# Edge counts in four quarters of a block, source one-hots in unwritten penalty slices, and attention columns formed after block 5

## The chip, the cores and the metric

The kernel runs on one core of one Trainium2 chip. The metric is the device time of one execution in microseconds (us). TensorE multiplies matrices, VectorE, ScalarE and GpSimd work on elements, and SyncE (SP) issues DMA transfers. Each engine takes its instructions in a fixed order of its own; semaphores tie the engines together.

## The reference

Two graph attention layers and a feed-forward part with residuals, over 1250 nodes of 768 features and 21250 edges sorted by target node:

```python
def gat_layer(x, W, att_src, att_dst, bias, src, dst, heads, out_ch, concat):
    h = (x @ W.T).reshape(n, heads, out_ch)
    a_src = jnp.einsum('nhc,hc->nh', h, att_src)
    a_dst = jnp.einsum('nhc,hc->nh', h, att_dst)
    e = jax.nn.leaky_relu(a_src[src] + a_dst[dst], 0.2)
    m = jax.ops.segment_max(e, dst, num_segments=n)
    ex = jnp.exp(e - m[dst])
    denom = jax.ops.segment_sum(ex, dst, num_segments=n)
    alpha = ex / (denom[dst] + 1e-16)
    out = jax.ops.segment_sum(alpha[:, :, None] * h[src], dst, num_segments=n)
...
x = x + gnn(layernorm(x), ...)    # gat 8 heads x 128, relu, gat 1 head x 768
x = x + ffn(layernorm(x)[None], ...)[0]
```

## The kernel before

The edge lists are turned into a dense matrix of counts: entry (target, source) says how many edges join the two. The 1250 nodes are ten blocks of 125 and the edges 170 chunks of 125, so that a block has 17 chunks (`CPB`) on average. For every chunk the kernel makes two one-hot matrices with one edge per partition: a source one-hot `of` over all 1250 nodes (VectorE, line 233) and a target one-hot `to` over the few nodes the chunk can reach (VectorE for the first 36 chunks; after that every third on GpSimd, line 249, the rest on ScalarE in two steps, lines 254 and 257). A matmul of `to` against `of` adds the chunk's edges to the counts of a block in PSUM (line 275).

Because the edges are sorted, a chunk touches only a few target nodes. `WINDOWS` (line 57) says which chunks are multiplied into which half of a block: two halves of 64 columns, 13 chunks each, laid over one another by a margin. One round of `count_block` (line 260) takes one chunk for each half, in three slices of the sources (512, 512 and 226); the two halves are two column tiles of TensorE's array. Edges outside their windows are counted (`n_out`, line 218), and if there is one, `count_all` (line 302) does all counts again without windows; with these inputs that branch is not taken, but all engines meet at it (line 558).

When a block's counts are complete, `use_count` (line 281) has ScalarE copy them to `full`, write the penalties `absent[:, b]` (zero where there is an edge, a huge number where there is none, line 286) and, after TensorE's transposes (line 297), the transposed counts `ct`. `absent` is one tile of ten slices of 1250 bf16 values, a slice for each block.

The softmax's maximum is found from the largest source term of each target: `top_of_block` (line 501) subtracts the penalties from a row of source terms and takes the maximum, one VectorE instruction for each head and block (line 503, which the profile lists as `unused<-rows,absent`). The rows of source terms come by way of memory: `a1p` (line 437) gives them for all heads, ScalarE copies them to `a1_row`, SP stores them to `as1_d` (line 446) and reads each head's row back, broadcast over partitions (line 492). The same `a1_row` is transposed into columns `a1` (lines 449 to 460: three transposes, five copies), from which `low_high` makes two scaled sets (line 480). The columns are first read by `load_destination_rows` and by the weights of the heads, all behind the branch.

The first stage runs: count block 0, layer norm and transposes of the ten blocks of `x`, `a1p`, the columns, and then for blocks 1 to 9 `count_block`, `h1_block(0, b)` (the features of heads 0 to 3, line 387) and the maxes named in `behind`. The `of` tiles rotate through 11 buffers, the `to` tiles through 13. The framework fixes the order on each engine when the kernel is built: it is not the program's order throughout, and maxes and one-hots are mixed on VectorE. Behind the branch come `load_destination_rows` for head 0 (its transpose `r_h_p`, line 465, and the copy `r_h_s`, line 467), four blocks of `h1` for heads 4 to 7, and the heads' loop, in which VectorE makes the weights (lines 527 and 531) and TensorE sums over sources (line 685).

Of the kernel before, what the change touches and what calls it, by code (L numbers as in the profile page):

```python
# [26 lines left out]
BF16 = mybir.dt.bfloat16  # L27
F16 = mybir.dt.float16
# [6 lines left out]
N = 1250  # L35
D = 768
E = 21250
H1, C1 = 8, 128
# [4 lines left out]
B = 125  # L43
NB = N // B
EC = E // B
# [7 lines left out]

CPB = EC // NB
MARGIN = 2
HALF = 64
WINDOWS = (
    (-MARGIN, -(-CPB * HALF // B) + MARGIN), (CPB * HALF // B - MARGIN, CPB + MARGIN)
)

NW = N + 128 - B + 1
# [4 lines left out]
def gnn_ffn(  # L66
# [25 lines left out]
    nc = tc.nc  # L92
# [15 lines left out]
    def ps_tr(name):  # L108
        return psum.tile([128, 512], F32, tag="tr", bufs=2, name=name)
# [16 lines left out]
    ep = pool("early", stack=early)  # L126
# [38 lines left out]
    first_i = ep.tile([B, NB, CPB], I32, name="first_i")  # L165
    last_i = ep.tile([B, NB, CPB], I32, name="last_i")

    def halves_of(r):

        return [  # L170
            2 * o + j for o in (-1, 0, 1) for j in range(2)
            if WINDOWS[j][0] <= r - CPB * o < WINDOWS[j][1]
        ]

    def start_of(half):
        return half // 2 * B + half % 2 * HALF

    for t, bounds in (
        (first_i, [start_of(halves_of(r)[0]) for r in range(CPB)]),
        (last_i, [start_of(halves_of(r)[-1] + 1) for r in range(CPB)]),  # L180
    ):
        c0 = 0
        for c1 in range(1, CPB + 1):
            if c1 == CPB or bounds[c1] != bounds[c0]:
                nc.gpsimd.iota(
                    t[:, :, c0:c1], pattern=[[B, NB], [0, c1 - c0]], base=bounds[c0],
                    channel_multiplier=0,
                )
                c0 = c1
# [3 lines left out]
    absent = marks.tile([B, NB, N], BF16, tag="marks", name="absent")  # L193
# [5 lines left out]
    ident = const.tile([128, 128], F32, name="ident")  # L199
# [8 lines left out]
    src_f = ep.tile([B, EC], F32, name="src_f")  # L208
# [17 lines left out]
    node = ep.tile([B, NW], F16, name="node")  # L226
# [1 line left out]
    minus_dst = ep.tile([B, EC], F32, tag="edge", name="minus_dst")  # L228
    nc.vector.tensor_scalar(minus_dst, dst_f, -1.0, None, op0=OP.mult)  # L229

    def one_hot(name, col, nodes, tag, bufs):
        t = ep.tile([B, nodes.shape[-1]], BF16, tag=tag, bufs=bufs, name=name)
        nc.vector.tensor_scalar(t, nodes, col, None, op0=OP.is_equal)  # L233
        return t


    hot = {}

    def hot_chunk(c):

        halves = [h + c // CPB * 2 for h in halves_of(c % CPB)]
        halves = [h for h in halves if 0 <= h < 2 * NB]
        of = one_hot(f"of{c}", src_f[:, c : c + 1], node[:, :N], "of", 11)
        n0 = start_of(halves[0])
        w = start_of(halves[-1]) + HALF - n0
        to = ep.tile([B, 3 * HALF], BF16, tag="to", bufs=13, name=f"to{c}")
        if c < 2 * CPB + MARGIN or c % 3 == 0:
            eng = nc.vector if c < 2 * CPB + MARGIN else nc.gpsimd
            eng.tensor_scalar(  # L249
                to[:, :w], node[:, n0 : n0 + w], dst_f[:, c : c + 1], None, op0=OP.is_equal  # L250
            )
            return of, to, n0
        away = ep.tile([B, 3 * HALF], F16, tag="away", bufs=1, name=f"away{c}")
        nc.scalar.activation(  # L254
            away[:, :w], node[:, n0 : n0 + w], AF.Abs, bias=minus_dst[:, c : c + 1], scale=1.0
        )
        nc.scalar.activation(to[:, :w], away[:, :w], AF.Relu, bias=ones, scale=-1.0)  # L257
        return of, to, n0

    def count_block(b):  # L260

        p = ps_count(f"count{b}")
        spans = [(max(0, CPB * b + lo), min(EC, CPB * b + hi)) for lo, hi in WINDOWS]
        for i in range(max(hi - lo for lo, hi in WINDOWS)):
            now = [(j, CPB * b + WINDOWS[j][0] + i) for j in range(2)]
            now = [(j, c) for j, c in now if spans[j][0] <= c < spans[j][1]]
            for _, c in now:
                if c not in hot:
                    hot[c] = hot_chunk(c)
            for c0 in range(0, N, 512):  # L270
                c1 = min(N, c0 + 512)
                for j, c in now:
                    of, to, n0 = hot[c]
                    o = start_of(2 * b + j) - n0
                    nc.tensor.matmul(  # L275
                        p[HALF * j : HALF * (j + 1), c0:c1], to[:, o : o + HALF], of[:, c0:c1],
                        start=(c == spans[j][0]), stop=(c == spans[j][1] - 1),
                    )
        use_count(p[:B, :N], b, f"w{b}", F16)

# [21 lines left out]
    def count_all():  # L302

        count = absent.bitcast(U16)
        nc.vector.memset(count, 0)
        with tc.For_i(0, EC, 1) as c:
            cols = ep.tile([B, 2], F32, name="cols")
            for i, t in enumerate((src_f, dst_f)):
                nc.vector.tensor_copy(cols[:, i : i + 1], t[:, bass.ds(c, 1)])
            of = one_hot("g_src", cols[:, 0:1], node[:, :N], "of", 11)  # L310
            to = one_hot("g_dst", cols[:, 1:2], node[:, :N], "of", 11)
            for b in range(NB):
                p = ps_count(f"g_count{b}")
                for c0 in range(0, N, 512):
                    c1 = min(N, c0 + 512)
                    nc.tensor.matmul(
                        p[:B, c0:c1], to[:, b * B : (b + 1) * B], of[:, c0:c1], start=True, stop=True
                    )
                nc.vector.tensor_tensor(count[:, b], p[:B, :N], count[:, b], OP.add)
        for b in range(NB):  # L320
            use_count(count[:, b], b, f"g{b}")
# [74 lines left out]
    for g in range(2):  # L396
        for h in range(H1):
            j = h % 4
            nc.tensor.matmul(
                vt[g][32 * j : 32 * j + 32, :384], att[:, h], w1n[h // 4][:, h % 4, g * 384 : (g + 1) * 384],  # L400
                start=(h < 4), stop=(h >= 4),
# [9 lines left out]
    p = ps_tr("vp")  # L411
    for k in range(KD):
        nc.tensor.matmul(
            p[:, 32 * k : 32 * k + 32], vt_s[:, k * 128 : (k + 1) * 128], pick_head,
            start=True, stop=True,
# [17 lines left out]
    spans = [(0, 3), (3, 6), (6, 8), (8, 10)]  # L433
    p = ps_mm("a1p")
    for k in range(KD):
        for j, (b0, b1) in enumerate(spans):
            nc.tensor.matmul(
                p[32 * j : 32 * j + 32, : (b1 - b0) * B], v[:, k], xt[:, k, b0 * B : b1 * B],
                start=(k == 0), stop=(k == KD - 1),
            )  # L440
    a1_row = ep.tile([128, 3 * B], F32, name="a1_row")
# [3 lines left out]
    for j, (b0, b1) in enumerate(spans):  # L445
        nc.sync.dma_start(
            as1_d[:, b0 * B : b1 * B], a1_row[32 * j : 32 * j + H1, : (b1 - b0) * B]
        )
    p = ps_tr("a1tp")
    a1 = const.tile([B, 2, H1, NB], F32, name="a1")  # L450
    for i in range(3):
        n = 128 if i < 2 else 64
        nc.tensor.transpose(
            p[:B, 128 * i : 128 * i + n], a1_row[:n, i * B : (i + 1) * B], ident[:n, :n]
        )
        pv = p[:B, 128 * i : 128 * i + n].rearrange("p (j c) -> p j c", c=32)[:, :, : 2 * H1]
        pv = pv.rearrange("p j (t h) -> p t h j", t=2)
        nc.vector.tensor_copy(a1[:, :, :, i : i + 4 : 3], pv[:, :, :, :2])
        if i < 2:
            nc.vector.tensor_copy(a1[:, :, :, 6 + i : 9 + i : 2], pv[:, :, :, 2:])  # L460

    def rows_to_dram(cols, n, name, sp):

# [8 lines left out]
    def low_high(a_s, shape, name):  # L472

        lo = const.tile(shape, F32, name=f"{name}_lo")
        nc.vector.tensor_scalar(lo, a_s, SLOPE, None, op0=OP.mult)
        hi = const.tile(shape, F32, name=f"{name}_hi")
        nc.vector.tensor_scalar(hi, a_s, 1.0 - SLOPE, None, op0=OP.mult)
        return lo, hi

    as1_lo, as1_hi = low_high(a1[:, 0], [B, H1, NB], "as1")  # L480


    class Head:
# [61 lines left out]
    def first_tops(blocks, hs=range(EARLY)):  # L545
        for b in blocks:
            for h in hs:
                top_of_block(heads[h], b)

    behind = {3: (0, 1), 4: (2,), 5: (3,), 6: (4,), 7: (5, 6), 8: (7,), 9: (8,)}  # L550
    for b in range(1, NB):
        count_block(b)
        if b == 1:
            h1_block(0, 0)
        h1_block(0, b)
        first_tops(behind.get(b, ()), range(4))
    first_tops(range(4), [4])
    with tc.If(n_val > 0):  # L558
        count_all()
# [115 lines left out]
    for h in range(H1):  # L675
        hd = heads[h]
        acc = [ps_mm(f"acc{h}_{g}") for g in range(NG)]
        for s in range(NB):
# [4 lines left out]
            for d in range(NB):  # L683
                g, j = divmod(d, PER)
# [3 lines left out]
                    start=(s == 0 and j == 0), stop=(s == NB - 1), skip_group_check=True,  # L688
# [26 lines left out]
    p = ps_mm("a2p")  # L715
# [13 lines left out]
    p = ps_tr("a2tp")  # L729
# [13 lines left out]
    first = marks.tile([128, NB * N // 2], F32, tag="marks", name="first")  # L743
    xn_first, first = first[:B, :D], first[:, D:]
    cls, first = first[:NCLS, :D], first[:, D:]
    gp, first = first[:NCLS, : 2 * D].rearrange("p (r d) -> p r d", r=2), first[:, 2 * D :]
    gjunk, first = first[:NCLS, :D], first[:, D:]
    cls_t, first = first[:, : KD * 32].rearrange("p (k j) -> p k j", k=KD), first[:, KD * 32 :]
# [82 lines left out]
    for q in range(NB // 2):  # L831
        pt = pt2[q]
        for i in range(2):
# [5 lines left out]
            for g, (c0, c1) in ((1, (384, D + 1)), (0, (0, 384))):  # L839
                for s in range(NB):  # L840
                    nc.tensor.matmul(  # L841
                        acc[g][:B, : c1 - c0], pt[:, s, i * B : (i + 1) * B], h2[:, s, c0:c1],
                        start=(s == 0), stop=(s == NB - 1),
# [4 lines left out]
            for g in (1, 0):  # L848
                c = slice(g * 384, (g + 1) * 384)
# [4 lines left out]
        c = slice(2 * q, 2 * q + 2)  # L854
# [102 lines left out]
    for k in range(KD):  # L957
        for a in range(4):
            nc.tensor.matmul(
                hp[32 * a : 32 * a + 32, :HID], cls_t[:, k], w_slots["in", a][:, k],  # L960
                start=(k == 0), stop=(k == KD - 1),
            )
    for k in range(KD):
        for m in range(KH):
# [3 lines left out]
                start=(k == 0), stop=(k == KD - 1),  # L968
# [111 lines left out]
```

## Time and profile before

Three executions took 792.51, 793.77 and 794.08 us; the median is 793.77. The profiled execution took 793.95 us, with a span of 792.2 us on its core from first to last instruction, at a mean granted TensorE clock of 0.997.

| | whole span |
|---|---|
| TensorE matmul busy | 755.1 us, 95% |
| TensorE weight load busy (beside matmuls) | 503.6 us, 64% |
| VectorE busy | 585.0 us, 74% |
| ScalarE busy | 325.4 us, 41% |
| GpSimd busy | 99.6 us, 13% |
| count matmuls, line 275, x768 | 82.7 us busy, 348 ns each |
| source one-hots, line 233, x170 | 85.1 us busy, 553 ns each |
| maxes over sources, line 503, 2 x 40 | 116.1 us busy, some 1452 ns each |
| `h1` matmuls, line 387, x240 | 114.1 us busy, 609 ns each |

A row of the page names the line, the engine and the operation, the tiles written and read, how often it ran, its busy time and the mean duration of one, and then the idle time of its engine just before it and what ended that. Durations of one instruction overlap those of the next, so neighbours can start closer together than they last. Matmuls in fp32 run as two passes, and each pass is an entry of its own.

### The profile page before, as it was taken

Reading aid. Unit: us, or ns where it says so; the run is one execution under the profiler, and the core shown is the slowest. Engines: PE = TensorE matmul, PEld = TensorE weight load, DVE = VectorE, ACT = ScalarE, POOL = GpSimd, SP = SyncE. Lnnn points to the kernel's source line nnn. Section 1 sums busy time; section 2 is a strip of 40 time slices with the busy share of each in tenths; the row PEclk is TensorE's granted clock in tenths of the full one; section 3 lists DMA queues with packets and bytes.
Section 4 is the critical chain, followed back from the end, with each engine's and each line's share of the span. In section 5 each row is a group of like instructions: output and inputs, shape, how many; then the busy total and the mean of one; then the engine's idle time right before and its main releaser. Section 6 shows DMA issues by size and latency. Waiting matters only on the chain.

```text
span 792.2 us, 10962 instructions
## 1 busy us (share of the span) xinstructions
PE 755.1 (95%) x4312; PEld 503.6 (64%) x4312; DVE 585.0 (74%) x1001; ACT 325.4 (41%) x573; POOL 99.6 (13%) x82
## 2 busy tenths in 40 slices
PE   4999999998989999899999999999999999999997
PEld 2554554553677787788787888555555555576765
DVE  7937999999999999999998785287946722251412
ACT  0886898860545455464546363201422400011000
POOL 1013554620000000000000000100010111023010
PEclk9999999999999999999999999999999999999999
DMA  7804000005202020422220100402110101093811
GB/s 242 286 13 154 1 2 1 1 2 211 98 1 66 1 99 1 145 80 66 82 66 1 66 1 1 152 0 68 60 40 19 40 19 40 0 311 111 326 39 41
DMA packets 21550, 58.45 MB, mean 74 GB/s; under 512 B 2385, under 2 KB 7627, under 8 KB 20344
## 3 DMA queue, kind: packets, MB, share of 16 engines
q1 hardware_dynamic: 21496, 57.72, 21.8%
q8 instruction: 35, 0.57, 0.3%
q14 instruction: 19, 0.16, 0.1%
HBM read 53.74 MB, written 3.98 MB: 73 GB/s over the span
## 4 chain that ended last, share of the span: by engine, by line
PE 48%; DVE 21%; issue 5%; ACT 3%; ACTq 0%; DVEq 0%
PE acc L841 15%; PE h2p L662 11%; DVE pt L527 9%; PE acc L685 7%; DVE pt L531 7%; PE f L906 5%; PE f L890 5%; DVE unused L503 4%; ACT on L607 1%; PE h1p L387 1%; PE a2p L718 1%; PE h1tp L610 1%; ACT pt L530 1%; PE xt2p L336 1%; PE candp L1003 1%
## 5 line engine op out<-in xcount | busy, mean ns | idle before, releaser
L530 ACT ACTIVATE pt<-pt,as_lo 125x1250 f32<-125x1250 f32 (+1 forms) x130 | 128.0, 1013 | 198.3 <-DVE pt L527 184.0
L685 PEld LDWEIGHTS acc<-g,pt 125*125 125x125 f32 x1600 | 185.6, 188 | 27.5 <-DVE pt L531 17.8
L685 PE MATMUL acc<-g,pt 125*125 125x129 f32 x1600 | 192.4, 275 | 9.3 <-DVE pt L531 9.2
L531 DVE SCALAR_TENSOR_TENSOR pt<-pt,ct 125x1250 f32<-125x1250 f32 (+1 forms) x130 | 133.3, 1051 | 9.1 <-ACT pt L530 8.9
L841 PE MATMUL acc<-h,pt 125*125 125x385 f32 (+1 forms) x400 | 129.7, 486 | 0.0
L527 DVE SCALAR_TENSOR_TENSOR pt<-rows_h,as_hi 125x1250 f32<-125x1250 f32 x80 | 119.9, 1510 | 5.8 <-PE acc L685 5.7
L387 PE MATMUL h1p<-w1s,xt 128*125 128x512 f32 x240 | 114.1, 609 | 2.9 <-DVEq L558 2.9
L841 PEld LDWEIGHTS acc<-h,pt 125*125 125x125 f32 x400 | 74.6, 187 | 53.9
L662 PE MATMUL h2p<-w2s,g 128*125 128x384 f32 x320 | 107.4, 487 | 0.0
L275 PE MATMUL count<-of,to 125*64 125x512 bf16 (+1 forms) x768 | 82.7, 348 | 5.7 <-DVE of L233 2.6
L233 DVE TENSOR_SCALAR of<-node,src_f 125x1250 bf16<-125x1250 f16 x170 | 85.1, 553 | 0.0
L662 PEld LDWEIGHTS h2p<-w2s,g 128*125 128x125 f32 x320 | 58.1, 188 | 37.7 <-issue 0.9
L275 PEld LDWEIGHTS <-to 125*64 125x64 bf16 x768 | 47.3, 111 | 45.0 <-issue 14.8
L387 PEld LDWEIGHTS h1p<-w1s,xt 128*125 128x125 f32 x240 | 42.1, 190 | 47.2 <-issue 47.1
L249 POOL TENSOR_SCALAR to<-node,dst_f 125x64 bf16<-125x64 f16 (+2 forms) x45 | 59.7, 1377 | 74.2 <-PE count L275 61.2
L503 DVE CUSTOM_DVE_ANT_0 unused<-rows,absent 125x1250 bf16<-125x1250 f32 x40 | 58.1, 1453 | 4.7 <-DMA rows<-as_d 3.9
L837 POOL TENSOR_TENSOR xb<-xb,b2r 125x768 f32<-125x768 f32 x10 | 18.2, 1818 | 327.9 <-DVE a_row L723 180.1
L503 DVE CUSTOM_DVE_ANT_0 unused<-srow_h,absent 125x1250 bf16<-125x1250 f32 x40 | 58.0, 1451 | 0.3
L910 DVE TENSOR_TENSOR o<-f,o 125x384 f32<-125x384 f32 x20 | 11.1, 557 | 52.5 <-PE f L906 30.3
L906 PE MATMUL f<-wf,gt 128*125 128x384 f32 x120 | 39.5, 486 | 0.0
L257 ACT ACTIVATE to<-away,ones 125x64 bf16<-125x64 f16 (+2 forms) x89 | 33.4, 375 | 10.5 <-PE count L275 7.1
L254 ACT ACTIVATE away<-node,minus_dst 125x64 f16<-125x64 f16 (+2 forms) x89 | 33.4, 375 | 10.5 <-DVE minus_dst L229 7.9
(175 smaller groups left out, 565.1 us busy)
## 6 DMA issues: line engine op xcount, KB each, us to landing
rows_h<-r_h_d SPq DMA_DIRECT2D x8, 1250.0 KB
w_more<-in_atom_in_t SPq DMA_DIRECT2D x3, 1152.0 KB
w_more<-in_atom_out_t SPq DMA_DIRECT2D x3, 1152.0 KB
x<-in_x SPq DMA_DIRECT2D x10, 336.0 KB
xb<-in_x SPq DMA_DIRECT2D x10, 336.0 KB
srow_h<-as_d SPq DMA_DIRECT2D x5, 625.0 KB
w1n<-in_w SPq DMA_DIRECT2D x2, 1536.0 KB
w1s<-in_w1t SPq DMA_DIRECT2D x2, 1536.0 KB
```

What stands on the lines that cost most here:

```text
L233: nc.vector.tensor_scalar(t, nodes, col, None, op0=OP.is_equal)
L249: eng.tensor_scalar(to[:, :w], node[:, n0 : n0 + w], dst_f[:, c : c + 1], None, op0=OP.is_equal)
L275: nc.tensor.matmul(p[HALF * j : HALF * (j + 1), c0:c1], to[:, o : o + HALF], of[:, c0:c1], start=(c == spans[j][0]), stop=(c == spans[j][1 ...
L387: nc.tensor.matmul(p[:B], xt[:, k, b * B : (b + 1) * B], w1s[g][:, k], start=(k == 0), stop=(k == KD - 1),)
L503: nc.vector.tensor_tensor_reduce(out=unused, in0=hd.src_row, in1=absent[:, b], scale=1.0, scalar=-ABSENT, op0=OP.subtract, op1=OP.max, acc ...
L527: nc.vector.scalar_tensor_tensor(o, hd.rows[:, 0, c0:c1], hi, hd.rows[:, 1, c0:c1], op0=OP.add, op1=OP.max)
L530: nc.scalar.activation(o, o, AF.Exp, bias=lo, scale=1.0)
L531: nc.vector.scalar_tensor_tensor(o, o, 1.0, ct[:, s, c0:c1], op0=OP.min, op1=OP.mult)
L662: nc.tensor.matmul(p[:B, :384], groups[i][:, h, b * B : (b + 1) * B], w2h[i][:, h, g * 384 : (g + 1) * 384], start=(h == 0), stop=(h == 3),)
L685: nc.tensor.matmul(acc[g][:B, j * (C1 + 1) : (j + 1) * (C1 + 1)], pt[:, d * B : (d + 1) * B], h1v[h // 4][:, h % 4, s, :], start=(s == 0 a ...
L841: nc.tensor.matmul(acc[g][:B, : c1 - c0], pt[:, s, i * B : (i + 1) * B], h2[:, s, c0:c1], start=(s == 0), stop=(s == NB - 1),)
L906: nc.tensor.matmul(p[:B, :384], gt[:, m, i, :], wf2[:, m, c], start=(m == 0), stop=(m == KH - 1),)
```

## The change

Three things are changed. A block's targets are counted in four quarters of 32 columns with windows of 9, 9, 10 and 8 chunks, each quarter a column tile of its own; a step takes one chunk for each quarter, and in later blocks the later quarters start one to three steps late. The source one-hots no longer rotate: `ring` has 12 places, and the slices of `absent` that are not yet written are places too, each until its block's counts are used; a plan made at build time gives each chunk the place whose last reader comes earliest. The `to` tiles are up to 96 columns wide instead of 192 and have 20 buffers. Last, the transposes, copies and scalings of the attention columns move from before the counting of block 1 to behind `h1_block(0, 5)` and the maxes that follow it.

```diff
-HALF = 64
-WINDOWS = (
-    (-MARGIN, -(-CPB * HALF // B) + MARGIN), (CPB * HALF // B - MARGIN, CPB + MARGIN)
+QUART = 32
+NQ = 4
+WINDOWS = tuple(
+    (CPB * QUART * j // B - MARGIN, min(CPB, -(-CPB * QUART * (j + 1) // B)) + MARGIN)
+    for j in range(NQ)
 )
...
+    def steps_of(b):
+        late = (0, 0, 0, 0) if b < 5 else (0, 1, 1, 2) if b < 7 else (0, 1, 2, 3)
+        spans = [(max(0, CPB * b + lo), min(EC, CPB * b + hi)) for lo, hi in WINDOWS]
+        steps = []
+        for i in range(max(hi - lo + n for (lo, hi), n in zip(WINDOWS, late))):
+            now = [(j, CPB * b + WINDOWS[j][0] + i - late[j]) for j in range(NQ)]
+            steps.append([
+                (j, c, c == spans[j][0], c == spans[j][1] - 1)
+                for j, c in now if spans[j][0] <= c < spans[j][1]
+            ])
+        return steps
+
+    steps = [(b, step) for b in range(NB) for step in steps_of(b)]
+    first_step, last_step, last_block = {}, {}, {}
+    for i, (b, step) in enumerate(steps):
+        for _, c, _, _ in step:
+            first_step.setdefault(c, i)
+            last_step[c], last_block[c] = i, b
+
+    ring = ep.tile([B, 12, N], BF16, name="ring")
+    places = [[-EC, NB - 1, absent[:, b], b] for b in range(NB)]
+    places += [[-EC, NB, ring[:, i], NB] for i in range(12)]
+    place_of = {}
+    for c in sorted(first_step, key=first_step.get):
+        place = min((p for p in places if last_block[c] <= p[3]), key=lambda p: p[:2])
+        place[0] = last_step[c]
+        place_of[c] = place[2]
     hot = {}
 
     def hot_chunk(c):
...
-        of = one_hot(f"of{c}", src_f[:, c : c + 1], node[:, :N], "of", 11)
...
-        to = ep.tile([B, 3 * HALF], BF16, tag="to", bufs=13, name=f"to{c}")
+        of = place_of[c]
+        one_hot(of, src_f[:, c : c + 1], node[:, :N])
...
+        to = ep.tile([B, 3 * QUART], BF16, tag="to", bufs=20, name=f"to{c}")
...
     def count_block(b):
 
         p = ps_count(f"count{b}")
...
-            for _, c in now:
+        for step in steps_of(b):
+            for _, c, _, _ in step:
                 if c not in hot:
                     hot[c] = hot_chunk(c)
             for c0 in range(0, N, 512):
                 c1 = min(N, c0 + 512)
-                for j, c in now:
+                for j, c, first, last in step:
                     of, to, n0 = hot[c]
-                    o = start_of(2 * b + j) - n0
+                    o = start_of(NQ * b + j) - n0
                     nc.tensor.matmul(
-                        p[HALF * j : HALF * (j + 1), c0:c1], to[:, o : o + HALF], of[:, c0:c1],
-                        start=(c == spans[j][0]), stop=(c == spans[j][1] - 1),
+                        p[QUART * j : QUART * (j + 1), c0:c1], to[:, o : o + QUART], of[:, c0:c1],
+                        start=first, stop=last,
                     )
...
+    def attention_columns():
+
+        p = ps_tr("a1tp")
+        for i in range(3):
+            n = 128 if i < 2 else 64
+            nc.tensor.transpose(
+                p[:B, 128 * i : 128 * i + n], a1_row[:n, i * B : (i + 1) * B], ident[:n, :n]
+            )
...
-
-    as1_lo, as1_hi = low_high(a1[:, 0], [B, H1, NB], "as1")
...
         h1_block(0, b)
         first_tops(behind.get(b, ()), range(4))
+        if b == 5:
+            attention_columns()
+            as1_lo, as1_hi = low_high(a1[:, 0], [B, H1, NB], "as1")
```

## The prediction

> **What bounds the kernel now.** I read the page's groups first, then busy time by window up to 182 us, VectorE's waits, and the timelines of VectorE and TensorE. The last instruction's chain is followed back no further than 182 us, to the branch at line 558, so the first stage has to be read from windows.
>
> ```profile
> core 0: us, PE busy (x) PEld busy (x) DVE busy (x) ACT busy (x) POOL busy (x), PEclk, DMA share, GB/s
> 46.90:63.80 16.90, 16.64 (x92) 8.19 (x90) 1.12 (x7) 11.13 (x24) 0.00 (x0) 1.00 0.28 90
> 63.80:182.10 118.30, 110.77 (x795) 58.53 (x794) 117.50 (x207) 93.86 (x206) 56.33 (x42) 1.00 0.05 19
> ```
>
> From 63.8 to 182.1 us VectorE is busy for 117.5 of 118.3 us; TensorE is nearly as full. Ahead of that lies a hole of 16.9 us in which VectorE works for 1.1. Its waits from 10 to 64 us name what fills the hole:
>
> ```profile
> DVE a L458 <- PE a1tp L453: 11.9, 3, 9.4
> DVE unused L503 <- DMA rows<-as_d: 3.9, 1, 3.9
> DVE rstd L354 <- ACT rstd L353: 2.7, 2, 1.6
> ```
>
> ```profile
> 45.89 1.00 DVE L233 TENSOR_SCALAR of<-node,src_f 125x1250 bf16<-125x1250 f16 x2
> 56.24 0.20 DVE L458 COPY a<-a1tp 125x32 f32<-125x32 f32 x1 [9.35 <-PE a1tp L453]
> 56.35 0.19 DVE L460 COPY a<-a1tp 125x32 f32<-125x32 f32 x1
> ...
> 59.78 0.20 DVE L477 TENSOR_SCALAR as_hi<-a 125x80 f32<-125x80 f32 x1
> 63.82 1.46 DVE L503 CUSTOM_DVE_ANT_0 unused<-rows,absent 125x1250 bf16<-125x1250 f32 x1 [3.85 <-DMA rows<-as_d]
> ```
>
> In its timeline VectorE has made 43 of the 170 source one-hots by 46.9 us. Then its queue holds the attention columns, which wait for transposes, and behind them the first max over sources, which waits for the DMA of the source rows. From 63.82 to 182.05 us it issues the other 127 one-hots and 40 maxes. Runs of one-hots start 0.485 us apart on average ("x15" at 67.56, next start 74.83; 13 from 127.17 to 133.47); 127 take 61.6 us, which leaves 1.41 us for a max. A block costs VectorE 17 x 0.485 + 4 x 1.41 = 13.9 us. TensorE spends 14.2: 78 count matmuls in 7.5 us (79.09 to 86.58) and 6.7 us of `h1` and transposes until the next count (86.58 to 93.29). After the branch VectorE again leads the chain until 334 us, so time won at the branch should reach the end.
>
> **Counting matmuls.** Windows of 9, 9, 10 and 8 chunks replace two of 13: an inner block has 36 x 3 = 108 matmuls for 78, in 10 steps (blocks 0 to 4), 11 (5, 6) or 12 (7 to 9) for 13 rounds. Single matmuls in the trace show a full-speed round taking 0.53 us: slices start 0.216, 0.216 and 0.094 us apart, both halves running together. Four column tiles at once are shown elsewhere:
>
> ```profile
> 729.62 0.50 PE L959 MATMUL hidp<-w_more,first 128*32 128x384 f32 x3
> 729.64 0.49 PE L959 MATMUL hidp<-w_in,first 128*32 128x384 f32 x1
> ...
> 730.27 1.49 PE L965 MATMUL hidp<-w_in,first 128*32 128x128 f32 x36
> ```
>
> Four matmuls on 32 columns go together, and 36 with their weight loads take 1.49 us, 41 ns a pair. So a step costs between 0.53 us (streaming) and 0.60 (four pairs at 41 ns in the 226-wide slice). I take 0.53: 5.3, 5.8 and 6.4 us a block, or 12.0, 12.5 and 13.1 with the 6.7. [...] Here the counting pairs already average 95 ns with their stalls, and line 965 has 41. I follow the rows: TensorE gains 1 to 2 us a block, which buys nothing while VectorE needs 13.9.
>
> **Places.** One-hot number and duration stay (125x1250, bf16 from f16, 553 ns). What changes is how far VectorE may run ahead: 11 buffers become 12 plus the unwritten `absent` slices, 22 in block 0 and 13 in block 9. The changed build's order has 52 one-hots before the first max, against 43, and no column copies between. Nine one-hots so move into the hole: 9 x 0.485 = **4.4 us** saved. The hole ends where it did, because the first max waits for the rows: last normalised block, `a1p`, its copy at 54.63, stores issued at 55.12, loads at 57.65, landing at 63.82. That path is ScalarE's. Block 0's counting ends some 0.8 us later (three thin steps follow the last chunk), but the changed order puts the square root before the `absent` and `ct` copies (1.34 and 1.26 us), so `shift` comes earlier. I keep 63.8, with 1.5 us either way.
>
> **Attention columns.** Their three transposes, five copies and two scalings move behind block 5's `h1`. The waits in the hole (11.9 us) yield nothing: the max still waits. The seven instructions, 0.11 us apart, now cost busy time: **+0.8**. Each later transpose waits for the copy before it and holds back the rest of block 6's counting. TensorE gets there near 116 us, VectorE near 119; TensorE stands about 3 us, VectorE about 0.4 for the third transpose (**+0.4**). Block 7 would then begin near 131, before VectorE needs its first freed places at about 132. SP issues the same DMAs in the same order; GpSimd keeps its 45 target one-hots and ScalarE its 89, at most 96 columns wide for 128, with 20 buffers for 13.
>
> **New waits.** A place is free when the step last reading it is done. I counted, for each one-hot, how many others lie between it and the last one which that step needs: 5 to 15 in blocks 1 to 4, and 3 to 5 for 25 in all, nearly all of them later. Behind a blocked one-hot stand maxes and further one-hots, and TensorE waits for those. No such wait is in this trace (VectorE has none but the rows' from 63.9 on). Lower end nothing, as four one-hots (1.9 us) cover three steps; upper end 0.3 us, half a step, for all 25, 7.5 us. I take **+0.5**, near the lower end, the trace's tight buffers not having stopped VectorE either.
>
> **After the branch.**
>
> ```profile
> DVE r_h_s L467 <- PE r_h_p L465: 1.5, 1, 1.5
> ```
>
> This transpose stood behind 14 `h1p` passes (182.29 to 190.07); in the changed order behind 10, and VectorE puts a max ahead of its copy. TensorE will have idled 7 us instead of 2.9, so passes may start slow: here, at granted clock 0.91, some start 0.86 us apart instead of 0.43. Between none and 1.5 us is saved; I take **-1.0**.
>
> **Sum.** -4.4 + 0.8 + 0.4 + 0.5 - 1.0 = -3.7 us. The profiled execution took 793.95 us (span 792.2), 0.18 above the median of 793.77; the forecast is 793.95 - 3.7 = 790.25, and from the median 790.1. I say **790.2**.
>
> **Rivals.** About 0.2% (1.6 us) is what a measurement can tell from no change: below 792.2 is faster, above 795.4 slower.
> - *Places gate VectorE* (slower). If the 25 close one-hots each wait 0.3 us, +7.5 replaces +0.5: 793.95 - 4.2 + 7.5 = 797.3. It cancels the gain from 0.17 us each. For it: places shrink to 13 and a step needs four chunks, three of them new at first. Against it: TensorE is up to 1.9 us a block faster than VectorE.
> - *The hole moves along* (no change). If block 0's later end and `shift` carry 2 us into the rows' arrival and the branch gives nothing: -4.4 + 0.8 + 0.4 + 0.5 + 2 = -0.7, 793.3. For it: VectorE idles in the hole anyway.
> - *The rows come early.* ScalarE's chain to `a1p` holds 2.4 us of waits, mostly for TensorE's transposes behind counts. If those go, as do the gates and the whole 1.5: -4.4 + 0.8 + 0.4 - 2.4 - 1.5 = -7.1, 786.9.
>
> **Chances.** Forecast 0.55 (own range 788.3 to 792.2), gated places 0.19, moved hole 0.14, early rows 0.12. The range is 786 to 797. Faster is the forecast and the early rows (0.66), no change the moved hole and the forecast's upper edge (0.15), slower the gated places (0.19).
>
> **What would show it.** Right: VectorE has 52 one-hots done by about 52 us, still idles until about 63.8, then runs without waits to a branch near 179; 108 count matmuls take 5.5 to 7 us; TensorE idles 5 to 8 us before the branch. Wrong: waits of one-hots on the count matmuls from block 5 on, a first max after 65.5, count blocks above 7.2 us (TensorE then passes 13.9), or `r_h_s` waiting over 1.5 us.

## The result and the profile after

The changed kernel took 794.65 us (median of 12 runs, 790.13 to 795.99), the kernel before 793.86 on the same chip (12 runs, 792.17 to 795.84). Over all runs of both the ratio is 1.0004, with a 95% interval of 0.9986 to 1.0022. (The ratios below are of this kind, always against the kernel before on the same chip; they are not the quotients of the medians.) Run again beside a later set of experiments it took 793.24 (21 runs, 791.38 to 796.05) against 793.92 (32 runs): 0.9999, interval 0.9989 to 1.0008. The change makes no difference that can be measured; 790.2 was forecast. The profiled execution took 795.88 us, with a span of 794.1 at a mean granted clock of 0.985, where before's had 0.997.

First the same two stretches as before the change: windows, with the busy time of each engine and the number of its instructions, and VectorE's waits up to 178 us.

```profile
core 0: us, PE busy (x) PEld busy (x) DVE busy (x) ACT busy (x) POOL busy (x), PEclk, DMA share, GB/s
46.90:62.90 16.00, 16.00 (x105) 8.36 (x105) 4.40 (x10) 14.61 (x34) 2.93 (x3) 1.00 0.21 61
62.90:178.10 115.20, 102.80 (x1042) 50.14 (x1040) 112.31 (x205) 85.58 (x199) 53.23 (x39) 0.98 0.09 35
```

```profile
DVE unused L532 <- DMA rows<-as_d: 11.6, 1, 11.6
DVE ring L234 <- PE count L302: 2.3, 2, 1.2
```

The first stage gained what was forecast, and more. The hole now holds 4.4 us of VectorE's work for 1.1, and what follows it takes 115.2 us for 118.3. VectorE waits for a place twice, not 25 times, 2.3 us in all. The branch is passed at 178.1 us for 182.0, and the first weights of head 0 start at 195.03 for 199.59. So 4.6 us were won at that point, and by the end they were gone. The table gives starts in us from the start of the trace (ends for the second and the last row), with the second trace of the changed kernel and one experiment beside it:

| | before | changed | changed, second trace | changed, order of before |
|---|---|---|---|---|
| first max | 63.82 | 62.93 | 61.22 | 61.41 |
| last max ahead of head 0's rows | 181.98 | 178.06 | 176.51 | 176.39 |
| first weights of head 0 | 199.59 | 195.03 | 193.47 | 194.69 |
| last `acc` matmul of head 3 | 343.09 | 345.44 | 340.99 | 338.22 |
| last `acc` matmul of head 7 | 498.39 | 500.58 | 496.13 | 493.53 |
| from the first weights to that | 298.80 | 305.55 | 302.66 | 298.84 |
| end | 792.16 | 794.10 | 789.69 | 787.05 |

The loss lies between the first weights and the end of head 3. From there to the end of head 7 the changed kernel takes 155.14 us and the kernel before 155.30. Windows over the ends of heads 0, 1 and 2, the changed kernel first, then before:

```profile
core 0: us, PE busy (x) PEld busy (x) DVE busy (x) ACT busy (x) POOL busy (x), PEclk, DMA share, GB/s
225.00:240.00 15.00, 10.88 (x81) 10.42 (x81) 14.03 (x16) 6.53 (x10) 0.00 (x0) 0.89 0.00 1
...
270.00:285.00 15.00, 13.21 (x81) 11.00 (x81) 13.53 (x21) 8.54 (x17) 0.00 (x0) 0.89 0.00 1
...
308.00:323.00 15.00, 13.15 (x81) 10.94 (x80) 13.37 (x21) 8.54 (x17) 0.00 (x0) 0.89 0.01 2
```

```profile
225.00:240.00 15.00, 12.52 (x99) 11.15 (x99) 15.00 (x17) 7.69 (x9) 0.00 (x0) 1.00 0.00 1
...
270.00:285.00 15.00, 13.58 (x96) 11.08 (x95) 14.73 (x19) 9.58 (x18) 0.00 (x0) 1.00 0.13 44
...
308.00:323.00 15.00, 13.33 (x93) 10.82 (x92) 14.74 (x20) 9.26 (x18) 0.00 (x0) 1.00 0.02 7
```

Before, the granted clock is 1.00 throughout and VectorE is busy for 14.7 to 15.0 of 15 us. After, the clock is 0.89 in each of the three windows, TensorE gets through 81 matmuls for 93 to 99, and VectorE, which had no holes here, idles 1 to 1.6 us. The clock records behind these numbers show half speed for exactly 3.41 us each time, from 231.6, 276.0 and 313.5 us. Each follows a pause of TensorE near the end of one head or the start of the next, as in this timeline of TensorE (start, duration, instructions, idle time before them and what ended it):

```profile
308.29 2.25 PE L717 MATMUL acc<-g,pt 125*125 125x129 f32 x19
312.40 0.93 PE L717 MATMUL acc<-g,pt 125*125 125x129 f32 x6 [1.85 <-DVE pt L560]
```

The three pauses are 2.32, 1.79 and 1.85 us. Before, the longest in heads 0 to 3 were 1.72, 1.62 and 1.42, and none was followed by half speed:

```profile
309.91 2.34 PE L685 MATMUL acc<-g,pt 125*125 125x129 f32 x16 [1.62 <-DVE pt L531]
```

There is a second difference. The code behind the branch is the same text in both kernels, but the build's scheduler, which starts from a changed first stage, put it in another order on VectorE, TensorE and ScalarE (on GpSimd it is equal). VectorE's time from the first weights to the last `pt` of head 3, added up from its instructions in each trace:

| us | before | changed |
|---|---|---|
| maxes for heads 5 to 7 | 23.3 (17) | 27.4 (20) |
| first passes of weights | 58.5 (41) | 57.3 (40) |
| second passes of weights | 55.5 (40) | 55.2 (40) |
| rest | 2.9 | 3.3 |
| idle | 0.8 | 4.1 |
| sum | 141.0 | 147.3 |

Three more maxes stand ahead of that point (counted from the branch 31 for 27), 4.1 us for 1.5 us less of weights, and VectorE idles 3.3 us more. Two causes are thus on the table: the order itself (theory O in the texts below), and the half speed of TensorE (theory C), which may only follow from it. A third would be that TensorE, nearly full, lets no gain through whatever the order (theory S).

### The profile page after: what moved, and what is told of

It reads as the page before. It is cut to its first block, busy times and chain, and to the rows that moved or that the text cites. A ratio compares the mean times of both kernels' runs of the same rounds, so it can differ in the third digit from the quotient of the medians.

```text
span 794.1 us, 11517 instructions
## 1 busy us (share of the span) xinstructions
PE 749.1 (94%) x4612; PEld 497.1 (63%) x4612; DVE 583.5 (73%) x1001; ACT 319.8 (40%) x573; POOL 99.0 (12%) x86
## 4 chain that ended last, share of the span: by engine, by line
PE 55%; DVE 18%; issue 3%; ACT 1%; DVEq 0%; ACTq 0%
PE acc L873 15%; PE acc L717 13%; PE h2p L694 11%; DVE pt L556 7%; DVE pt L560 5%; PE f L938 5%; PE f L922 5%; DVE unused L532 4%; PE h1tp L642 1%; PE h1p L415 1%; PE a2p L750 1%; PE xt2p L364 1%; PE candp L1035 1%; PE hidp L991 1%; ACT pt L559 0%
## 5 line engine op out<-in xcount | busy, mean ns | idle before, releaser
L717 PEld LDWEIGHTS acc<-g,pt 125*125 125x125 f32 x1600 | 189.4, 191 | 28.5 <-DVE pt L560 17.5
L717 PE MATMUL acc<-g,pt 125*125 125x129 f32 x1600 | 196.4, 278 | 10.5 <-DVE pt L560 10.3
L302 PE MATMUL count<-ring,to 125*32 125x512 bf16 (+1 forms) x729 | 63.7, 342 | 3.0 <-DVE to L279 2.0
L279 POOL TENSOR_SCALAR to<-node,dst_f 125x64 bf16<-125x64 f16 (+3 forms) x45 | 58.2, 1483 | 62.1 <-PE count L302 44.3
L302 PEld LDWEIGHTS <-to 125*32 125x32 bf16 x1068 | 35.7, 96 | 46.3 <-issue 14.9
L234 DVE TENSOR_SCALAR ring<-node,src_f 125x1250 bf16<-125x1250 f16 x116 | 59.2, 545 | 2.3 <-PE count L302 2.3
L302 PE MATMUL count<-absent,to 125*32 125x512 bf16 (+1 forms) x339 | 52.1, 355 | 3.7 <-DVE absent L234 1.9
L942 DVE TENSOR_TENSOR o<-f,o 125x384 f32<-125x384 f32 x20 | 11.1, 557 | 52.5 <-PE f L938 30.2
L287 ACT ACTIVATE to<-away,ones 125x64 bf16<-125x64 f16 (+4 forms) x89 | 31.1, 350 | 12.9 <-PE count L302 9.4
```

Of the source, the lines that this page charges most:

```text
L279: eng.tensor_scalar(to[:, :w], node[:, n0 : n0 + w], dst_f[:, c : c + 1], None, op0=OP.is_equal)
L302: nc.tensor.matmul(p[QUART * j : QUART * (j + 1), c0:c1], to[:, o : o + QUART], of[:, c0:c1], start=first, stop=last,)
L717: nc.tensor.matmul(acc[g][:B, j * (C1 + 1) : (j + 1) * (C1 + 1)], pt[:, d * B : (d + 1) * B], h1v[h // 4][:, h % 4, s, :], start=(s == 0 a ...
```

## The experiments

**The order, transplanted.** Both kernels trace the same instructions behind the branch, so the order of one can be laid on the other: edges that fix the order of issue, and nothing else, between neighbours on VectorE, TensorE and ScalarE. Chained in its own order, the changed kernel gives the same instructions in the same order on every engine, so that the chain itself adds nothing.

```diff
+ORDER = {
+    "DVE": (
+        "0-1 4 2 5 24 3 6-7 25 58 26-27 59 8 60 9 61 91 10 92 11-15 17 19-20 16 18 21-22 28 31 23 "
...
+def chain(tc, warm=()):
...
+        for a, b in zip(full, full[1:]):
+            tc.add_manual_dep(by_name[b], a, info, reason="order")
```

> The changed kernel; what VectorE, TensorE and ScalarE issue after the branch is chained in the order of the kernel before, nothing else differs. Theory O (order): the first stage's 3.9 us are lost because the new build issues the same instructions after the branch in another order (by the end of head 3, 35 maxes ahead of the weights for 30 before); with the old order they come through: 789.5 to 790.5 us, acc0 to acc7 all some 4 us earlier than before. Theory C (clock): the loss is the halved TensorE clock in the heads, which follows TensorE's idle stretches of 1.8 us and more; those belong to the new order, so also 789.5 to 790.5, and a granted clock of 0.99 or more in every run. Theory S (second bound): TensorE bounds the heads whatever the order, and a gain at the branch cannot come through: 793.5 to 795.

> The kernel before; what VectorE, TensorE and ScalarE issue after the branch is chained in the changed kernel's order, nothing else differs. Theory O: it loses what the order costs, some 4.5 us, in every run: 797.5 to 799. Theory C: the loss is only as large as the halvings it draws, 0 to 5 us: 793.5 to 799 with a wide spread that follows the granted clock. Theory S: the order is without effect, 793.5 to 794.5.

(The 35 and 30 maxes of the first text include four and three semaphore waits on the maxes' line; the maxes alone are 31 and 27.)

The changed kernel in the order of before took 790.48 us (5 runs, 788.83 to 791.09), 0.9966 of before, interval 0.9953 to 0.9979: the gain that was forecast. The stretch from the first weights to the end of head 7 is 298.84 us, as before the change, 298.80. The kernel before in the changed order took 799.68 (4 runs), 1.0087, interval 1.0072 to 1.0101, somewhat above the 797.5 to 799 of theory O; its trace has two halved windows in the heads, and 303.92 us for the stretch. So the order decides whether the gain reaches the end, in both directions, and TensorE's own work does not forbid it: theory S falls.

**The half speed, taken away alone.** The changed order is kept; TensorE gets small matmuls where it pauses.

```diff
+            if h < 4 and (s == 9 or (s == 1 and h > 0)):
+                for _ in range(FILL):
+                    nc.tensor.matmul(
+                        acc[0][:B, 387:512], ident[:B, :B], ident[:B, :125],
+                        start=False, stop=False, skip_group_check=True,
+                    )
```

> The changed kernel in its own order; four matmuls of 125 columns, on the identity, into columns of acc that nobody reads, stand ahead of the first matmul of step 9 of heads 0 to 3 and of step 1 of heads 1 to 3, where TensorE waits 1.8 to 2.3 us for VectorE. They fill about 1 us of each wait. Theory C: no halved window is left in heads 0 to 3 and the time is 789.5 to 791. Theory O: the clock is even, but VectorE has the same instructions in the same order, so 793.5 to 795.

Windows of this run, laid where the three of the changed kernel were:

```profile
223.60:238.60 15.00, 12.27 (x107) 11.77 (x106) 14.98 (x17) 7.80 (x14) 0.00 (x0) 1.00 0.00 2
268.60:283.60 15.00, 14.94 (x111) 12.62 (x110) 14.89 (x22) 9.32 (x18) 0.00 (x0) 1.00 0.03 8
303.90:318.90 15.00, 14.34 (x106) 12.03 (x105) 14.37 (x21) 8.25 (x17) 0.00 (x0) 1.00 0.01 2
```

The clock is 1.00, and VectorE's idle time up to the last `pt` of head 3 is 0.76 us for 4.08, with the same instructions in the same order. The stretch to the end of head 7 is 302.84 us: 2.7 less than the 305.55 of the changed kernel's first trace, 4.0 more than with the order of before. But the 4.0 are not the order's alone, because one of the fillings has a cost. In head 3 TensorE does not pause ahead of step 9, and there the four matmuls (line 779, eight passes) hold up the last step of the head:

```profile
337.70 0.60 PE L724 MATMUL v2p<-w2n,att2c 128*2 128x256 f32 x4
338.23 1.14 PE L779 MATMUL acc<-ident 125*125 125x125 f32 x8
339.20 2.37 PE L786 MATMUL acc<-g,pt 125*125 125x129 f32 x20
```

In the changed kernel's second trace `acc` follows `v2p` directly. From VectorE's last `pt` of head 3 to the end of that head the filled kernel takes 4.24 us, the changed kernel 3.37 in the first trace and 3.36 in the second, the kernel before 2.77. Up to that last `pt` the filled kernel's VectorE idles no longer than that of the kernel before (0.76 and 0.77 us), and the times from the first weights are 141.0 us before, 143.7 filled and 147.3 changed. By this reckoning the order costs 2.7 us on VectorE and 0.6 behind it, some 3.1 us by the end of head 7, and the half speed of the first trace 3.6.

The time was 792.62 us (14 runs, 791.42 to 794.57), 0.9995, interval 0.9984 to 1.0005. Theories C and O each gave a number, and it fell between. By the timed medians alone this run can't be told from the unfilled kernel; the split is read from the traces.

> The changed kernel itself once more, beside the next three on the same chip. Theory O (order and halvings): 794 to 795.5 us, and run by run the time falls with the granted clock, 790 to 791.5 at 0.991 and above, 794.5 to 796 at 0.987 and below. Rival (the earlier median was that chip's): a median under 793.5.

The median was 793.24 us: the rival's figure, and not theory O's 794 to 795.5. Run by run the time does fall with the granted clock. 13 of the 21 runs had 0.991 and took 791.38 to 793.62 us (forecast 790 to 791.5), 4 at 0.986 or 0.987 took 794.40 to 794.80, and 4 at 0.983 to 0.985 took 795.72 to 796.05. The median is lower than the first because more of these runs had a high clock; the first set had 8 of 12 at 0.987 or below. Whether the chip has a part in that was not tried. A window of 3.41 us at half speed lowers the mean clock of a 794-us run by 0.0021, so 0.991 and 0.984 lie three windows apart and some 3.4 us: 1.1 us for a window. The traces agree with that in size: with one, two and three halved windows in the heads the changed order takes 302.66 us (second trace), 303.92 (laid on the kernel before) and 305.55 (first trace) to the end of head 7, and without one, by the split above, some 302.0.

**Which part of the order.** If the three or four maxes that stand early were all of it, moving them back should suffice; if VectorE's queue were, its order alone should.

> The changed kernel in its own order after the branch, with one thing moved: VectorE's maxes for heads 4 to 7 stand where the kernel before has them among the weights (by the last weights of head 3, 27 maxes for 31; of head 6 and 7 two each stay earlier, where their u needs them). TensorE and ScalarE keep the changed order. Theory M (it is the maxes): four of 1.45 us leave the stretch in which VectorE is the bound, 5.6 us less there, and heads 4 and 5 take them up: 790 to 791.5 us. Theory R (it is the rest of the order: rec, h1 passes, transposes): 793.5 to 795. Theory C (the clock alone): the time follows the granted clock, 790 at 0.993 or above and 794 at 0.987.

> The changed kernel; after the branch VectorE alone issues in the order of before, TensorE and ScalarE keep the changed kernel's. Theory V (VectorE's own order sets the heads, since it bounds them): 790.5 to 792. Theory E (the three engines' orders fit one another, and an order of one against the others opens new waits, as the moved maxes did at 803): 795 or more, with waits of pt for ScalarE's exp or of acc for pt in heads 0 to 4.

They took 803.14 (4 runs) and 809.56 us (5 runs), ratios of 1.0119 (1.0099 to 1.0138) and 1.0200 (1.0187 to 1.0213): both worse than either whole order. The first lies above the ranges of all its three theories, the second is as theory E had it. VectorE's waits in heads 0 to 3, with the maxes moved and then with VectorE's order of before:

```profile
DVE pt L642 <- ACT pt L641: 6.4, 6, 1.3
DVE pt L638 <- PE acc L799: 1.8, 3, 1.0
```

```profile
DVE pt L638 <- PE acc L799: 9.7, 4, 2.9
DVE r_h_s L580 <- PE r_h_p L578: 4.2, 2, 2.9
```

A max stands between the two passes of a weight and covers ScalarE's `Exp`, 1.34 us, that the second pass waits for. Take it away and the wait is bare. With VectorE alone in the old order, the `pt` buffers come free late, because TensorE reads them by another plan. So the maxes are not the whole cause, and an order of one engine is only good against the orders of the others. The early maxes also fit with nothing being given back later: from the last `pt` of head 3 to that of head 5 the kernel before and the filled one take 76.8 and 76.9 us, but VectorE idles 0.4 us in the one and 4.0 in the other. The filled one has fewer maxes left there (9 for 13), yet is no faster, so that VectorE is not its bound in those heads.

**The parts of the change, one by one,** all with the order of before behind the branch, so that 790.48 us, or 0.9966 of before (0.9953 to 0.9979), is the mark. Columns formed at their old place:

```diff
-        if b == 5:
-            attention_columns()
-            as1_lo, as1_hi = low_high(a1[:, 0], [B, H1, NB], "as1")
```

> The changed kernel with the order of before after the branch (790.5 us), and the attention columns formed where the kernel before forms them, in the hole ahead of the first max; 52 one-hots still stand ahead of that max. Theory P (the prediction's terms): the columns' 0.8 us on VectorE and 0.4 us of waits go back into the hole: 789.1 to 789.6, and the branch is passed 1.2 us earlier. Rival: the columns ahead of the max make it later than 62.9 us, or cost nothing where they stand now: 790.5 or more.

789.25 us (6 runs, 788.13 to 790.92), 0.9942, interval 0.9925 to 0.9959, which overlaps the mark's. The time lies in the range of theory P, but in the trace its 1.2 us are not there: the last max ends at 177.24 us for 176.39. TensorE now pauses 2.04 us at 83.5, and half speed follows from 86.8. What the columns' place is worth is not settled.

```diff
-QUART = 32
-NQ = 4
+QUART = 64
+NQ = 2
...
-        late = (0, 0, 0, 0) if b < 5 else (0, 1, 1, 2) if b < 7 else (0, 1, 2, 3)
+        late = (0, 0)
```

> The changed kernel with the order of before after the branch (790.5 us), counting in two halves of 64 columns as before (12 buffers of target one-hots for 20), places and columns as changed; 51 one-hots ahead of the first max. Theory P: counting is beside VectorE's 13.9 us a block, so quarters buy nothing: 790.2 to 791. Rival Q: with halves TensorE needs 14.2 us a block again, 0.3 to 0.5 us more than VectorE, which the quarters had taken away: 792.5 to 794.

791.69 us (14 runs, 790.12 to 792.63), 0.9977, interval 0.9967 to 0.9986: between the two forecasts, and not told apart from the mark. Up to `r_h_s` the traces show a gain and a price that cancel. With quarters the branch comes 1.9 us earlier (176.7 for 178.6), 1.2 of which the first max already has. But TensorE then idles 7.6 us ahead of the branch for 1.0, its clock is halved for three windows, and `r_h_s` starts at 185.5 us for 185.2. In the heads this trace of the halves loses 1.6 us more, with a pause of TensorE of 2.46 us and a halved window from 202.6 us in head 0. So quarters are not shown to be worth anything here, nor to be worth nothing.

```diff
-    places = [[-EC, NB - 1, absent[:, b], b] for b in range(NB)]
-    places += [[-EC, NB, ring[:, i], NB] for i in range(12)]
+    places = [[-EC, NB, ring[:, i], NB] for i in range(12)]
```

> The changed kernel with the order of before after the branch (790.5 us), its source one-hots in the ring of 12 alone, none in the slices of absent; 45 one-hots ahead of the first max for 52. Theory P: seven fewer in the hole cost 7 x 0.485 = 3.4 us: 793.5 to 794.3, the branch at 180 us or later. Rival: the one-hots in the hole are not what brought the branch forward, 790.5.

With 12 places, 20 one-hots take a place whose last reader comes in the same step or the next, so that a part of the counts is taken from the wrong chunk. It took 796.75 us, above the 793.5 to 794.3 of theory P (7 runs), 1.0038, interval 1.0025 to 1.0052, and the last max ends at 184.7 us, 8.3 later than with `absent` for 3.4 forecast (2.2 of that already at the first max, behind a halved window from 28.8 us). Its VectorE waits up to 186 us, and those of the kernel with all places:

```profile
DVE ring L293 <- PE count L360: 6.2, 8, 1.5
```

```profile
DVE ring L293 <- PE count L361: 2.4, 2, 1.4
```

This is the prediction's rival of gated places, 8 waits of up to 1.5 us, and the slices of `absent` are what keeps it away. So they are worth more than the seven one-hots in the hole; how much a kernel would lose in which those 20 one-hots wait for their readers is open.

**TensorE kept busy ahead of the branch,** in the changed order, in the order of before, and with the columns at their old place:

```diff
+    last = [x for x in tc.nc.cur_bb.bb.instructions if type(x).__name__ == "InstMatmult"]
+    with tc.issue_after(last[-1]), tc.issue_after(last[-7]):
+        p = ps_mm("warm")
+        for i in range(26):
+            nc.tensor.matmul(p[:B, :125], ident[:B, :B], ident[:B, :125], start=(i == 0), stop=(i == 25))
```

> The changed kernel in its own order; 26 matmuls of 125 columns on the identity fill some 6 of the 7.6 us in which TensorE idles ahead of the branch. The three halved windows at 173.6 to 183.8 us should go. Theory C: the ten h1 passes behind the branch take 2.7 us less; that is worth 0 to 2.7 us at the end, 792 to 794.7. Theory O: VectorE's maxes cover that stretch, no gain, 794 to 795.

> The changed kernel with the order of before after the branch (790.5 us), and 26 matmuls on the identity in the 7.6 us in which TensorE idles ahead of the branch. Theory H (the three halved windows behind the branch slow 14 h1 passes and hold back r_h_s, for which VectorE waits 2.2 us there): the wait goes, the first weights come 2 to 3 us earlier, 787.8 to 788.7. Rival: VectorE's maxes or the DMA of the rows take up the gain, 790 to 791.

> The same with the attention columns formed where the kernel before forms them. Theory H and the prediction's terms: a further 1.2 us, 786.6 to 787.6, the fastest of all, with a granted clock of 0.995 or more. Rival: the columns' place is worth nothing once TensorE stays at full clock, 788 to 789.

In the changed order it is worth nothing: 793.24 us (22 runs), 1.0004, interval 0.9992 to 1.0016, and the first weights start at 193.55 for 193.47 in the second trace. In the order of before it took 788.83, just above theory H's range (6 runs, 787.15 to 791.07), 0.9938, interval 0.9923 to 0.9954, the lowest median of all, though its interval just touches the mark's. VectorE's wait behind the branch, without and with the 26 matmuls:

```profile
DVE r_h_s L557 <- PE r_h_p L555: 2.2, 1, 2.2
```

```profile
DVE r_h_s L557 <- PE r_h_p L555: 1.5, 1, 1.5
```

The wait shrank by 0.7 us and did not go: the last 1.9 us of the pause stayed open, and in this trace drew one halved window. The third kernel took 790.16 (11 runs, 787.85 to 793.77), 0.9959, interval 0.9942 to 0.9976, above both forecasts, so the further 1.2 us did not come; its trace too has a pause of 2.03 us and half speed at 87.6, and one more halved window from 29.6.

## Why the prediction was wrong

The mechanism forecast for the first stage was there. What failed is the path behind the branch, in one sentence of the prediction, that VectorE "again leads the chain until 334 us, so time won at the branch should reach the end". Its sum has no term for what the changed order does to the heads.

- **Counting matmuls.** Right where it can be read: in blocks 2 to 5 and 7, 108 take 5.5 to 7.1 us (8.2 in block 6, with the columns' transposes among them) for 5.3 to 6.4 forecast, 51 to 66 ns a pair. In blocks 8 and 9 counts and `h1` are mixed on TensorE.
- **Places.** The one-hots came as forecast: the 52nd starts at 50.8 us. From the first to the last max the trace has 115.1 us for 118.2, 3.0 less; the terms for places, columns and waits came to 2.7. That the sum fits is in part luck, for singly they are not confirmed: waits for places took 2.3 us for 0.5, and the columns' 1.2 could not be recovered.
- **The hole's end.** Mis-sized. It was kept at 63.8 with 1.5 us either way; in the second trace the first max starts at 61.2. The copy of `a1p` is 0.5 us earlier, and the first row lands 4.1 us after its load is issued for 6.2. Why it lands sooner is open: with the columns back, with halves and with 12 places alone it still took 4.0 to 4.1 us, so none of the three parts alone brings it about. The first trace, with a halved window from 30.2 us, had 62.9, which hid this.
- **After the branch.** The time from the last max to `r_h_s` fell by 0.7 us, 8.40 to 7.74, for 1.0. The idle TensorE ahead of the branch (7.6 us, forecast 5 to 8) and the slow passes behind it came as written: ten take 7.22 us from 178.38, at a clock of 0.50 up to 183.8. What was not asked is where else a TensorE with more slack would pause.
- **The step that failed.** The prediction put the cost of the changed order in the heads at nothing, without a reason. In the first trace 6.75 us were lost from the first weights to the end of head 7: some 3.1 to the new order itself, 3.6 to half speed, which followed the longer pauses of that order (2.32, 1.79 and 1.85 us, for 1.72 at most before). In the second trace it was 3.8, with one halved window in the heads for three. The order was open to reading beforehand: it was read as far as `r_h_p`, where it was put at a gain of 1.0 us, and not through the heads.
- **The forecast and the kernel in the order of before.** Its 790.48 us comes near the 790.2, but not by the forecast's sum: in its trace the first max comes 2.4 us earlier, which the forecast did not count, and the time from the last max to `r_h_s` grows from 8.40 to 9.10 us, where 1.0 less was forecast. The agreement of the two numbers is in part luck.
- **The rivals.** Places did not gate VectorE, the hole did not move along, and the rows did come early, by 2.6 us for 2.4, without any gain at the end. The time landed with none of these mechanisms.

## What to carry to other kernels

Where a scheduler orders the build, a change in one stage is also a change of the order in every stage behind it: compare the orders to the end, and count what stands ahead of each milestone on the engine that bounds. To tell an order from a change, lay the old order on the new code. Where two engines are both nearly full, work pulled forward on one need not be given back when the bound passes to the other (it was not here), and TensorE's idle share says little about its clock: between 225 and 240 us the kernel before kept TensorE busy for 12.52 of 15 us at a clock of 1.00, between 270 and 285 the changed one for 13.21 at 0.89. Half speed in its heads stood behind single pauses of 1.79 to 2.32 us, and the share does not show those.

## What the runs showed of the hardware

In the first trace of the changed kernel half speed begins at five points ahead of the program's end: at 30.2, 173.6, 231.6, 276.0 and 313.5 us. It lasts 10.24 us at the second of them and 3.41 at each of the others. In the trace of the kernel before it begins once, at 183.4 us, and lasts 3.41. In the 3.41 us ahead of these points the clock was 1.00, and TensorE idled 2.32, 2.81, 2.19, 1.79 and 1.85 us in the changed kernel and 2.31 us in the kernel before. The third of the five begins 0.1 us ahead of the end of its pause, the fourth and fifth 1.2 and 1.1 us behind it.

The length of a pause alone did not tell which one half speed would follow: in the same trace it followed the pause of 1.79 us that ends at 274.73, and not the one of 1.80 us that ends at 238.89; the clock is 1.00 from 235.0 to 275.9. In the kernel before it did not follow the 1.72, 1.62 and 1.42 us of heads 0 to 3, with a clock of 1.00 from 186.8 to 790.0.

The same program also differed from one execution to the next. The second trace, at a mean granted clock of 0.991 for 0.985, has one halved window in the heads for three, and the 21 runs beside it spread from 0.983 to 0.991. What decides it was not shown. That this makes the changed kernel's spread over 790 to 796 us, and its two medians 1.4 us apart, is argued from the granted clocks: of the runs without a trace the single stretches at half speed are not on record.
